# Spreading the normalisation factors of layer 1's first pass: 32 transposed rows and picking products in place of a widened copy

## The chip, the cores and the metric

The kernel runs on one core of a Trainium2 chip. The time is device time in microseconds (us), from one execution of the whole program; the number given for a kernel is the median of its runs. A core has engines that run side by side, each with its own queue of instructions in order: TensorE (PE in the profile; PEld is its loading of weights), VectorE (DVE), ScalarE (ACT), GpSimd (POOL), and SyncE (SP), which issues the transfers here. They wait for each other through semaphores.

## The reference

The input x is (4, 64, 256, 256) in fp32: four images, 64 channels, 256 rows and columns. Layer 0 is a gated convolution with a small Fourier filter; layer 1 runs two state-space blocks over the pixels, one along rows and one along columns. What the change concerns is the entry of layer 1, where each pixel is normalised over its 64 channels, once for each of the two directions, with the same mean and variance and different gains:

```python
def _layer_norm(x, g, b):
    mu = jnp.mean(x, axis=-1, keepdims=True)
    var = jnp.mean((x - mu) ** 2, axis=-1, keepdims=True)
    return (x - mu) * jax.lax.rsqrt(var + EPS) * g + b

def _s5_block(x, i, ...):
    fx = _layer_norm(x, ln1_g[i], ln1_b[i])
    h = _s5_scan(fx, ...)          # a linear recurrence along the sequence, both ways
    x = jax.nn.gelu(h) + fx
    fx2 = _layer_norm(x, ln2_g[i], ln2_b[i])
    return fx2 @ ff_enc[i].T @ ff_dec[i].T + fx2

x = x + layer0(_gn(x))             # _gn: normalisation over groups of 2 channels
x = x + layer1(_gn(x))             # y_h over rows, y_v over columns, then a 1x1 fusion
```

So one factor, rsqrt(var + EPS), belongs to each pixel, and it multiplies all 64 channels of that pixel.

## The kernel before

Layer 0 takes the first 4.18 ms of the profiled execution. Layer 1 then handles the four images one after the other. For each it runs `pass_a`, `scan` and `pass_b`. `pass_a` normalises the image, stores the result in DRAM for `pass_b`, and forms the summaries of 16 pixels that `scan` turns into carried states.

`pass_a` cuts an image into 16 strips of 16 rows (NS1 = 16). A strip lies in SBUF as 128 partitions (64 channels of one half of the rows, 64 of the other) by 8 rows of 256 pixels, and is worked on as four blocks i = 0 to 3 of 512 columns. The steps of a strip are these, with the names that the profile shows:

- `centre(g, i)`: a product of the block with the matrix `cenr` takes out the mean over the channels (PSUM tile `pc`, two banks). ScalarE copies it to `xc` and squares it to `sq`.
- `sums`: products of `sq` with a narrow matrix write the variances into PSUM tile `pv`, as 32 columns of TensorE for each block. ScalarE copies them to `sums`.
- `rstd_of`: four transposes bring them to 128 pixels by 32 (again `pv`; two factors for each of 4 x 4 pieces), VectorE adds EPS (`ve`), and GpSimd raises them to the power -1/2 (`rs`, 128 x 32).
- `widen`: one VectorE copy repeats each of the 32 factors 64 times, once for each channel: `rw`, 128 x 2048, one buffer.
- `affine(g, i)`: four transposes of 128 x 128 pieces of `rw` lay the factors out as channels by pixels (PSUM tile `pr`, two banks), and VectorE multiplies them with `xc` into `z`.
- `scaled_in`: ScalarE applies the gains and biases of the two directions (`fv`, `fh`); `store` sends both to DRAM.
- `mirrored`, `summary_columns`, `summary_rows`, `place_columns`, `place_rows`: sums and differences of mirrored pixels (`sd`, by VectorE for one direction and GpSimd for the other), products with `wa` (PSUM tiles `pt` and `ps`), a copy `m` by ScalarE, and VectorE's writes into the states `sf` and `sb`.

The order of work on each engine is written out by hand. The loop over n runs 20 times and mixes the steps of five strips: `centre` works on strip n, `sums`, `rstd_of` and `widen` on strip n - 1, `affine` on strip n - 2, the rest on strips n - 3 and n - 4. Nothing is reordered, since `tc.keep_in_program_order` fixes each engine's order. At the end of an iteration stand

```python
                at(n - 2, affine, 3)
                ...
                at(n - 3, summary_columns, n - 3, 0)
                at(n - 1, widen)
                at(n - 3, mirrored, 0)
```

and the next iteration begins with `centre(n, 0)` and `affine(n - 2, 0)`, which reads what `widen` wrote just before. On TensorE a steady iteration is: `pc`, `pr`, `pv` (sums), `pt`, `pc`, `pr`, `pv` (transposes), `ps`, `pc`, `pr`, `ps`, `pc`, `pr`, `pt`. An fp32 product is two TensorE instructions in the profile (two passes over the moving columns), a transpose is one.

In the profile's lines, L1096 is the helper that records a product, L1100 the one that records a transpose, and L301 and L162 are the helpers behind nearly all VectorE, ScalarE and GpSimd operations in order, so those are told apart by their tiles.

Of the kernel before, what the change touches and what calls it, by code (L numbers as in the profile page):

```python
# [16 lines left out]
C = 64  # L17
HID = 170
S = 256
P = 128  # L20
# [88 lines left out]
def tile_kernel(ctx: ExitStack, tc: tile.TileContext, x, cst, w0, winp, wdwp, w1, out):  # L109
    nc = tc.nc  # L110
    nb = x.shape[0]

    def new(pool, shape, tag, bufs=None, dt=F32):
        return pool.tile(shape, dt, tag=tag, name=tag, **({} if bufs is None else {"bufs": bufs}))
# [9 lines left out]
    def con(name):  # L124
        o, w = CONST_AT[name]
        return ct[:, o : o + w] if o < CONST_0 else tables[0][:, o - CONST_0 : o - CONST_0 + w]

    ident, swap, nswap = con("ident"), con("swap"), con("nswap")
# [6 lines left out]
    def group_norm(mv, psum, tag, keep, bank=(512,)):  # L135

        ps = new(psum, [P, *bank], tag)
        ps = ps[:, 0] if len(bank) > 1 else ps
        nc.tensor.matmul(ps[:, 0:1], lhsT=con("gm"), rhs=mv[:, 0:1], start=True, stop=True)
        nm = new(gpool, [P, 1], f"nm{keep}")  # L140
        nc.vector.tensor_scalar(nm, ps[:, 0:1], -1.0, None, ALU.mult)
        dev = new(gpool, [P, 1], "dev")
        nc.vector.tensor_tensor(dev, mv[:, 0:1], nm, ALU.add)
        var = new(gpool, [P, 1], "var")
        nc.vector.scalar_tensor_tensor(var, dev, dev, mv[:, 1:2], ALU.mult, ALU.add)
        ps2 = new(psum, [P, *bank], tag)
        ps2 = ps2[:, 0] if len(bank) > 1 else ps2
        nc.tensor.matmul(ps2[:, 0:1], lhsT=con("gm"), rhs=var, start=True, stop=True)
        ve = new(gpool, [P, 1], "ve")
        nc.vector.tensor_scalar(ve, ps2[:, 0:1], GN_EPS, None, ALU.add)  # L150
        rs = new(gpool, [P, 1], f"rs{keep}")
        nc.gpsimd.tensor_tensor(rs, ve, mhalf[:, 0:1], ALU.pow)
        return nm, rs
# [10 lines left out]
    vec, act, gps = InOrder(nc.vector), InOrder(nc.scalar), InOrder(nc.gpsimd)  # L164
# [27 lines left out]
    with ExitStack() as l0:  # L192
        wp = l0.enter_context(tc.tile_pool(name="w0", bufs=1))
# [16 lines left out]
        for h in range(2):  # L210
            p = slice(h * C, (h + 1) * C)
# [39 lines left out]
        with tc.tile_pool(name="pssp", bufs=1, space=PSUM) as pp:  # L251
            ps = new(pp, [P, 512], "sp")
# [23 lines left out]
        with ExitStack() as l1w:  # L276
# [31 lines left out]
            vec = Paced()  # L308
# [3 lines left out]
            def tmp(n=2, dt=F32):  # L312
                n_tmp[0] += 1
                return new(sp, [P, n], f"tmp{n_tmp[0]}", None, dt)
# [49 lines left out]
            def mul(a, b):  # L364
                o = tmp()
                TT(o, a, b, ALU.mult)
                return o
# [76 lines left out]
            for d in range(2):  # L444
# [28 lines left out]
                if d == 1:  # L473
# [18 lines left out]
                    for f in range(2):  # L492
                        o = wtb[1][:, at_e + 8 * f : at_e + 8 * f + 8].rearrange("p a (h c) -> p (a h) c", h=2)
                        group(o, 16, c1[f], c2[f], ec_r, ec_i, place)
                else:
# [6 lines left out]
                    for f in range(2):  # L502
                        o = wtb[0][:, at_r + 8 * f : at_r + 8 * f + 8].rearrange("p a (h c) -> p (a h) c", h=2)
# [40 lines left out]
            u, t, r, i = mul(ur, ur), mul(ui, ui), tmp(), tmp()  # L544
# [9 lines left out]
            n = 1  # L554
# [26 lines left out]
            for d in range(2):  # L581
                w = lambda name, d=d: wts[d][:, W1_AT[name][0] : W1_AT[name][0] + W1_AT[name][1]]
                ps = new(pw, [P, 512], "pw")
# [9 lines left out]
            for d in range(2):  # L593
                ps = new(pw, [P, 512], "pw")
# [7 lines left out]
                for h in range(2):  # L602
                    p = slice(h * C, (h + 1) * C)
                    TS(wos[d][p, p], mts[d][p, 0, :], par(d, "g2")[p], None, ALU.mult)
            burst[1]()
            for d in range(2):
                mm(
                    psb[:, 0:1], lhsT=mts[d][0:C].rearrange("p h c -> p (h c)"), rhs=par(d, "b2")[0:C],
                    start=(d == 0), stop=(d == 1),
                )  # L610
                ps = new(pw, [P, 512], "pw")
# [14 lines left out]
        pp = l0.enter_context(tc.tile_pool(name="ps0", bufs=2, space=PSUM))  # L626
        wk = l0.enter_context(tc.tile_pool(name="wk0", bufs=2))
# [316 lines left out]
        for b in range(nb):  # L944
            if b + 1 < nb:
                nxt_stats = new(wk, [P, 2 * NS0, 6], "stats1")
            for s in range(NS0):
                n = b * NS0 + s
# [116 lines left out]
    def load_strip(b, s):  # L1065
        t = new(ring, [P, 8, S], "strip")
        for h, r, row in rows_of(s):
            nc.sync.dma_start(out=t[h, r], in_=x1d[b][:, row : row + 7 : 2, :])
        return t
# [3 lines left out]
    with tc.tile_pool(name="psn", bufs=2, space=PSUM) as pn:  # L1073
        for b in range(nb):
            nm, rs = group_norm(moments2[b], pn, "pn", "1")
# [3 lines left out]
            ps = new(pn, [P, 512], "pn")  # L1079
# [3 lines left out]
    def pass_a(b, x0):  # L1083
        with ExitStack() as es:
            wp = es.enter_context(tc.tile_pool(name="wa", bufs=1))
            wk = es.enter_context(tc.tile_pool(name="wka", bufs=2))
            pp = es.enter_context(tc.tile_pool(name="psa", bufs=2, space=PSUM))
# [3 lines left out]
            rs, off = norms[:, b, 0:1], norms[:, b, 1:2]  # L1091
            cen = new(wp, [P, P], "cenr")
            nc.vector.tensor_scalar(cen, con("cen"), rs, None, ALU.mult)

            def mm(*args, **kw):
                tc.keep_in_program_order(nc.tensor.matmul(*args, **kw))  # L1096

            def turn_blocks(ps, v):
                for k in range(4):
                    tc.keep_in_program_order(nc.tensor.transpose(ps[:, k * P : (k + 1) * P], v(k), ident))  # L1100

            def centre(g, i):
                ps = new(pp, [P, 512], "pc")
                mm(ps, lhsT=cen, rhs=g["x"][:, 2 * i : 2 * i + 2, :].rearrange("p a b -> p (a b)"), start=True, stop=True)
                xc, sq = new(wk, [P, 512], "xc", 10), new(wk, [P, 512], "sq", 5)
                act.activation(xc, ps, AF.Identity, bias=off)
                act.activation(sq, ps, AF.Square, bias=off)
                g["xc", i], g["sq", i] = xc, sq

            def sums(g):  # L1110

                ps = new(pp, [P, 512], "pv", 1)
                for i in range(4):
                    mm(ps[32 * i : 32 * i + 32], lhsT=con("on2")[:, 2:34], rhs=g.pop(("sq", i)), start=True, stop=True)
                g["sums"] = new(wk, [P, 512], "sums", 1)
                act.copy(g["sums"], ps)
# [7 lines left out]
                gps.tensor_tensor(r, ve.rearrange("p n c -> p (n c)"), mhalf, ALU.pow)  # L1124
                g["rs"] = r

            def widen(g):

                g["r"] = new(wk, [P, 32, C], "rw", 1)
                vec.tensor_copy(g["r"], g.pop("rs").unsqueeze(2).to_broadcast([P, 32, C]))  # L1130

            def affine(g, i):

                if i == 0:
                    g["fv"], g["fh"] = new(wk, [P, 8, 256], "fv"), new(wk, [P, 16, 128], "fh")
                ps, z = new(pp, [P, 512], "pr"), new(wk, [P, 2, 16, 16], "z", 3)
                turn_blocks(ps, lambda k: g["r"][:, 8 * k + 2 * i : 8 * k + 2 * i + 2].rearrange("p a c -> p (a c)"))
                vec.tensor_tensor(
                    z.rearrange("p r q g -> p r g q"), g.pop(("xc", i)).rearrange("p (r g q) -> p r g q", r=2, q=16),
                    ps.rearrange("p (r g q) -> p r g q", r=2, q=16), ALU.mult,  # L1140
                )
                g["z", i] = z
# [23 lines left out]
            def summary_columns(g, s, k):  # L1166
                if k == 0:
                    g["pc"] = new(pp, [P, 512], "pt", 1)
                ps, sd = g["pc"], g.pop(("sd", 1, k))
                for r in range(4):  # L1170
                    mm(
                        ps[:, k * 256 : (k + 1) * 256], lhsT=wa[1][:, k * 4 + r], rhs=sd[:, r], start=(r == 0),
                        stop=(r == 3),
                    )
                if k == 1:
                    g["mc"] = new(wk, [P, 256], "m")
                    act.copy(g["mc"], ps[:, 256:])
# [34 lines left out]
            def at(s, step, *args):  # L1212
                if 0 <= s < NS1:
                    step(got[s], *args)

            for n in range(NS1 + 4):
                if n + 1 < NS1:
                    got[n + 1] = {"x": load_strip(b, n + 1)}
                at(n, centre, 0)
                at(n - 2, affine, 0)  # L1220
                at(n - 1, sums)
                at(n - 2, scaled_in, 0)
                at(n - 3, mirrored, 1)
                at(n - 4, summary_columns, n - 4, 1)
                at(n, centre, 1)
                at(n - 2, affine, 1)
                at(n - 1, rstd_of)
                at(n - 2, scaled_in, 1)
                at(n - 4, place_columns, n - 4)
                at(n - 4, summary_rows, n - 4, 0)  # L1230
                at(n, centre, 2)
                at(n - 2, affine, 2)
                at(n - 2, scaled_in, 2)
                at(n - 4, summary_rows, n - 4, 1)
                at(n, centre, 3)
                at(n - 2, affine, 3)
                at(n - 4, place_rows, n - 4)
                at(n - 2, scaled_in, 3)
                at(n - 2, store, n - 2)
                at(n - 3, summary_columns, n - 3, 0)  # L1240
                at(n - 1, widen)
                at(n - 3, mirrored, 0)

    def scan(tabs):
# [299 lines left out]
    for b in range(nb):  # L1544
        pass_a(b, first)
        first = pass_b(b)
# [77 lines left out]
```

## Time and profile before

| What | us |
|---|---|
| Median of 3 runs (lowest to highest) | 9118.38 (9117.01 to 9126.76) |
| The profiled execution's own time | 9128.26 |
| Its span, first to last instruction | 9126.5 |
| Granted TensorE clock, mean | 0.986 of full |
| Stretches with the four `pass_a` (each with some us around it) | 318, 306, 290, 315 |
| TensorE busy in them | 256.7, 246.5, 246.2, 257.8 |
| TensorE idle ahead of the transposes of `rw`, all four | 181.2 |
| 64 copies into `rw`, median of one | 3.234 |

The profile is of one execution, which took 9.9 us more than the median run. A TensorE matmul's end in it is modelled, and neighbouring matmuls overlap, so times of TensorE work are best read from one start to the next. Busy shares are averages over stages with different limits; the stage that matters here is `pass_a`, some 1.2 ms in all.

### The profile page before, as it was taken

How to read it: one execution, taken by the hardware profiler on the slowest of the kernel's cores; microseconds unless marked ns; L12 is line 12 of the kernel's file. 1: busy time of each engine (PE TensorE's matmuls, PEld its weight loads, DVE VectorE, ACT ScalarE, POOL GpSimd, SP SyncE). 2: the span in 40 equal slices, each digit the busy share in tenths (PEclk: the TensorE clock that was granted, in tenths of full speed). 3: DMA queues.
4: the chain of work that ended last, by engine and by line, in shares of the span. 5: the costliest groups of instructions: out<-in, count | busy, mean ns of one | idle time of the engine just before them, and what ended most of it. 6: DMA issues, size and time to landing. Idle time of an engine off the chain costs nothing. (4 is left out here: it accounts for less than half of the span.)

```text
span 9126.5 us, 182410 instructions
## 1 busy us (share of the span) xinstructions
PE 8613.1 (94%) x78454; PEld 5705.4 (63%) x78454; DVE 7105.8 (78%) x8837; ACT 3460.7 (38%) x5218; POOL 2406.8 (26%) x1278
## 2 busy tenths in 40 slices
PE   3999999999999999998899988999978999889999
PEld 2666666666666666665566656566655666555666
DVE  7999999999999998896766756677756677567676
ACT  3444444444444444445422236222254222352222
POOL 3000000000000000003734435544446444455443
PEclk9999999999999999999999999999999999999999
DMA  7444444444444333334423335233253233451332
GB/s 175 107 107 107 104 105 110 109 103 105 108 107 107 92 93 87 91 85 134 147 57 88 85 103 177 73 80 88 70 170 113 70 89 80 117 187 40 88 84 70
DMA packets 655573, 938.37 MB, mean 103 GB/s; under 512 B 43184, under 2 KB 584880, under 8 KB 619184
## 3 DMA queue, kind: packets, MB, share of 16 engines
q1 hardware_dynamic: 654768, 926.71, 38.3%
q8 instruction: 618, 10.13, 0.5%
q14 instruction: 187, 1.53, 0.1%
HBM read 583.86 MB, written 275.05 MB: 94 GB/s over the span
## 5 line engine op out<-in xcount | busy, mean ns | idle before, releaser
L205 PE MATMUL m<-v,sw 64*128 64x256 f32 (+1 forms) x8192 | 1538.6, 392 | 0.1
L205 PEld LDWEIGHTS m<-v,sw 64*128 64x128 f32 (+1 forms) x8192 | 1120.0, 187 | 503.2 <-issue 360.0
L1439 POOL TENSOR_TENSOR xr<-xr,fx 128x512 f32<-128x512 f32 x512 | 651.5, 1272 | 1864.4 <-ACT xr L1438 1375.5
L1344 PE MATMUL pst<-fx,wb 64*128 64x256 f32 (+1 forms) x4992 | 1019.8, 438 | 37.8 <-DVE stm L301 18.3
L692 POOL MEMSET at<- 64x256 f32 x4 | 1.2, 308 | 3685.1 <-PE two L205 3685.1
L301 DVE SCALAR_TENSOR_TENSOR acc<-xat,taps,acc 128x1024 f32<-128x1024 f32 x640 | 820.6, 1282 | 15.3 <-ACT acc L162 1.6
L1344 PEld LDWEIGHTS pst<-fx,wb 64*128 64x128 f32 (+1 forms) x4992 | 508.9, 187 | 374.6 <-issue 245.3
L1469 POOL TENSOR_TENSOR rs<-ve,mhalf 128x32 f32<-128x32 f32 x128 | 695.5, 5434 | 100.5 <-DVE ve L301 100.5
L162 ACT ACTIVATE ge<-two 128x1024 f32<-128x1024 f32 x256 | 262.7, 1026 | 1080.1 <-PE two L205 1080.0
L301 DVE SCALAR_TENSOR_TENSOR stm<-stm,step,pst 128x512 f32<-128x512 f32 x640 | 478.6, 748 | 232.5 <-PE pst L1344 219.0
L1440 ACT ACTIVATE sq<-xr 128x512 f32<-128x512 f32 x512 | 323.4, 632 | 876.4 <-POOL xr L1439 876.4
L205 PEld LDWEIGHTS m<-ct,hw 128*64 128x64 f32 x16384 | 509.3, 138 | 118.1 <-issue 118.1
L301 DVE SCALAR_TENSOR_TENSOR sto<-sto,step,pst 128x512 f32<-128x512 f32 x512 | 382.9, 748 | 242.5 <-PE pst L1344 231.2
L1344 PE MATMUL px<-wb,xr 128*128 128x128 f32 x4096 | 567.8, 282 | 0.0
L301 DVE TENSOR_TENSOR z<-xc,pr 128x512 f32<-128x512 f32 x256 | 265.1, 1037 | 386.2 <-PE pr L1100 378.8
L301 DVE TENSOR_TENSOR hw<-two,wsp 128x1020 f32<-128x1020 f32 (+1 forms) x384 | 422.7, 1101 | 176.0 <-PE two L205 162.7
L1344 PEld LDWEIGHTS px<-wb,xr 128*128 128x128 f32 x4096 | 518.0, 192 | 54.2 <-issue 41.8
L301 DVE TENSOR_TENSOR y<-px,rs 128x512 f32<-128x512 f32 x512 | 354.2, 692 | 226.5 <-PE px L1344 217.2
L1344 PE MATMUL ph<-sto,wb 128*64 128x128 f32 (+1 forms) x5120 | 528.0, 299 | 0.0
L205 PE MATMUL m<-ct,hw 128*64 128x64 f32 x16384 | 527.1, 223 | 0.0
L1344 PE MATMUL ph<-stm,wb 128*64 128x128 f32 (+1 forms) x5120 | 525.0, 299 | 0.0
L1344 PEld LDWEIGHTS ph<-stm,wb 128*64 128x64 f32 (+1 forms) x5120 | 408.9, 147 | 144.6 <-issue 128.0
(317 smaller groups left out, 16420.7 us busy)
## 6 DMA issues: line engine op xcount, KB each, us to landing
strip<-x1d SPq DMA_DIRECT2D x512, 256.0 KB, 7.5
fx<-fxd SPq DMA_DIRECT2D x128, 1024.0 KB, 7.0
at<-in_x_dram SPq DMA_DIRECT2D x248, 320.0 KB, 5.4
xen<-xat SPq DMA_DIRECT2D x256, 258.0 KB, 4.8
sx<-in_x_dram SPq DMA_DIRECT2D x256, 256.0 KB, 4.0
pr<-in_x_dram SPq DMA_DIRECT2D x256, 256.0 KB, 4.1
er<-in_x_dram SPq DMA_DIRECT2D x256, 256.0 KB, 4.1
x1d<-x SPq DMA_DIRECT2D x256, 256.0 KB, 4.0
```

The source lines that it names most:

```text
L162: return lambda *args, **kw: tc.keep_in_program_order(getattr(self.engine, name)(*args, **kw))
L205: tc.keep_in_program_order(nc.tensor.matmul(*args, **kw))
L301: tc.keep_in_program_order(getattr(nc.vector, name)(*args, **kw))
L692: nc.gpsimd.memset(at[C:P, 4, 1 : S + 1], 0.0)
L1344: tc.keep_in_program_order(nc.tensor.matmul(*args, **kw))
L1439: nc.gpsimd.tensor_tensor(xr, xr, fx, ALU.add)
L1440: nc.scalar.activation(sq, xr, AF.Square)
L1469: nc.gpsimd.tensor_tensor(r, ve.rearrange("p n c -> p (n c)"), mhalf, ALU.pow)
```

## The change

`widen` and the tile `rw` are gone. In their place `lay` transposes the factors once, from 128 pixels x 32 to 32 rows x 128 pixels (PSUM tile `pv`), and ScalarE copies that to the new tile `rt` (32 x 128). `affine` then no longer transposes; it forms four products per block. The stationary operand is a slice of a constant `pick`, 32 rows by 128 columns, that holds a one where a channel's column belongs to the row in question, and the moving operand is `rt`. Each product thereby copies two of the 32 rows to 64 channels each, into the same place of `pr` as before. `pick` is written once at the start of each `pass_a` by a VectorE copy of a 32 x 32 identity, spread 64 times.

The place in the order changes too: `lay` stands ahead of `summary_columns(n - 3, 0)`, where `widen` stood behind it. In the built program TensorE's steady iteration reads: `pc`, `pr`, `pv` (sums), `pt`, `pc`, `pr`, `pv` (transposes), `ps`, `pc`, `pr`, `ps`, `pc`, `pr`, `pv` (the new transpose), `pt`. ScalarE's new copy stands between the last `fh` of one iteration and the first `xc` of the next.

```diff
             cen = new(wp, [P, P], "cenr")
             nc.vector.tensor_scalar(cen, con("cen"), rs, None, ALU.mult)
 
+            pick = new(wp, [32, 32, C], "pick")
+            nc.vector.tensor_copy(pick, ident[0:32, 0:32].unsqueeze(2).to_broadcast([32, 32, C]))
+
@@
-            def widen(g):
-
-                g["r"] = new(wk, [P, 32, C], "rw", 1)
-                vec.tensor_copy(g["r"], g.pop("rs").unsqueeze(2).to_broadcast([P, 32, C]))
+            def lay(g):
+
+                ps = new(pp, [P, 512], "pv", 1)
+                tc.keep_in_program_order(nc.tensor.transpose(ps[0:32, :P], g.pop("rs"), ident))
+                g["r"] = new(wk, [32, P], "rt")
+                act.copy(g["r"], ps[0:32, :P])
@@
                 ps, z = new(pp, [P, 512], "pr"), new(wk, [P, 2, 16, 16], "z", 3)
-                turn_blocks(ps, lambda k: g["r"][:, 8 * k + 2 * i : 8 * k + 2 * i + 2].rearrange("p a c -> p (a c)"))
+                for k in range(4):
+                    o = 8 * k + 2 * i
+                    mm(
+                        ps[:, k * P : (k + 1) * P], lhsT=pick[:, o : o + 2].rearrange("p a c -> p (a c)"), rhs=g["r"],
+                        start=True, stop=True,
+                    )
@@
                 at(n - 2, scaled_in, 3)
                 at(n - 2, store, n - 2)
+                at(n - 1, lay)
                 at(n - 3, summary_columns, n - 3, 0)
-                at(n - 1, widen)
                 at(n - 3, mirrored, 0)
```

## The prediction

> **What bounds the kernel now.** I read the groups of TensorE first, then the tile `rw`, then one steady iteration of `pass_a` in order of time, then the clock by stretches. The page's first rows and the groups by form:
>
> ```profile
> PE 8613.1 (94%) x78454; PEld 5705.4 (63%) x78454; DVE 7105.8 (78%) x8837; ACT 3460.7 (38%) x5218; POOL 2406.8 (26%) x1278
> ...
> L1100 PE MATMUL pr<-ct,rw 128*128 128x128 f32 x1024 | 168.3, 290 | 181.2 <-DVE rw L301 181.0
> ```
>
> TensorE is the fullest engine, and in `pass_a` its one large idle place is ahead of these transposes: 181 us over 64 strips, ended by VectorE's copy. The same in time order (start, length, what, idle before):
>
> ```profile
> 4290.84 1.02 PE L1096 MATMUL pc<-strip,cenr 128*128 128x512 f32 x2
> 4294.37 0.63 PE L1100 MATMUL pr<-ct,rw 128*128 128x128 f32 x4 [2.51 <-DVE rw L301]
> 4294.93 1.06 PE L1096 MATMUL pv<-sq,ct 128*32 128x512 f32 x8
> ...
> 4297.76 1.02 PE L1096 MATMUL pc<-strip,cenr 128*128 128x512 f32 x2
> 4298.62 0.60 PE L1100 MATMUL pr<-ct,rw 128*128 128x128 f32 x4
> 4299.05 0.60 PE L1100 MATMUL pv<-ct,sums 128*128 128x128 f32 x4
> 4299.58 2.06 PE L1096 MATMUL ps<-sd,wa 64*128 64x128 f32 x32
> 4301.57 1.12 PE L1096 MATMUL pc<-strip,cenr 128*128 128x512 f32 x2
> 4302.53 0.60 PE L1100 MATMUL pr<-ct,rw 128*128 128x128 f32 x4
> 4303.06 2.06 PE L1096 MATMUL ps<-sd,wa 64*128 64x128 f32 x32
> ...
> 4306.01 0.60 PE L1100 MATMUL pr<-ct,rw 128*128 128x128 f32 x4
> 4306.44 1.89 PE L1096 MATMUL pt<-sd,wa 128*128 128x256 f32 x8
> 4308.17 1.02 PE L1096 MATMUL pc<-strip,cenr 128*128 128x512 f32 x2
> ```
>
> Three things are to be seen. An iteration takes 4308.17 - 4290.84 = 17.33 us; without the wait it is dense. The wait, from start to start, is 4294.37 - 4290.84 - 0.86 (a `pc` without one, 4297.76 to 4298.62) = 2.67, so TensorE's own work is 14.66. And a change of array shape costs: four transposes take 0.43 where the next group has the same shape (4298.62, 4306.01) but 0.53 ahead of the 64-row `ps` (4299.05, 4302.53), and a `pc` takes 0.96 behind a `ps` against 0.86: 0.10 to leave a shape plus 0.10 in the first instruction of the next, 0.20 per change. Six changes are in the 14.66.
>
> The wait has a second price. Clock by stretches of 3.41 us (PE busy first, PEclk the sixth figure):
>
> ```profile
> 4256.03:4259.44 3.41, 1.37 (x12) 0.58 (x12) 2.60 (x2) 0.76 (x2) 0.81 (x1) 1.00 1.00 402
> 4259.44:4262.86 3.42, 3.42 (x11) 2.50 (x8) 2.50 (x3) 2.00 (x3) 0.00 (x0) 0.50 1.01 315
> 4262.86:4266.27 3.41, 3.41 (x36) 2.67 (x36) 1.68 (x4) 2.25 (x4) 0.54 (x1) 1.00 0.25 47
> ```
>
> A stretch mostly filled by the wait is followed by one at half clock, which costs about 1.65 us. By the starts of the 64 `rw` copies, each pass has two short first intervals (12.7 to 14.2), twelve middle ones and one last. Of the 48 middle ones 32 take about 17.33 and sixteen 18.7 to 19.0; together 857.5 us, mean 17.86. The last ones take 17.25, 14.63, 17.51 and 17.45.
>
> **What the Trainium skill says.** TensorEngine Tiling (Array Packing), Key Properties: changing the tiling mode, not just the tile, drains TensorE. The trace agrees: the 0.20 above. TensorE: Matmul & The Clock Gate, Why this matters for your kernels: one product over 32 rows takes as long as one over 128. No run here has 32 rows; 64-row `ps` pairs take (2.0 - 0.2)/16 = 0.11 a pass, like 128 rows. The same page, What's actually happening: the clock halves after a free-running window of 3413 ns without enough work. The windows shown agree. TensorEngine Tiling, Feature Incompatibilities: column tiling and the fp32 transpose mode exclude each other. The new transpose has 32 output rows; nothing here shows one.
>
> **The change, part by part,** for a steady iteration.
>
> *Copy and wait.* VectorE loses 3.23 us, which matters only through the wait; -2.67 on TensorE, and the half-clock windows behind it.
>
> *Transposes to products.* A transpose is one instruction, 0.109 (0.43/4). An fp32 product of this size is two: in the last pass `px`, four such products, has
>
> ```profile
> 4752.60 1.05 PE L1344 MATMUL px<-wb,xr 128*128 128x128 f32 x8
> 4753.49 0.60 PE L1462 MATMUL pv<-ct,sums 128*128 128x128 f32 x4
> ```
>
> 0.89 for eight, 0.112 each. Four groups an iteration: 4 x (0.896 - 0.436) = +1.84.
>
> *Changes of shape.* The products use 32 rows. Changes per iteration become 13: `pc` to `pr` four times, `pr` to each follower four times, sums to `pt`, transposes to `ps`, two `ps` to `pc`, new transpose to `pt`. Seven more, 7 x 0.20 = +1.40. The trace has no 32-row group, so this is bounded by 0 (no drain) and 0.20; I take 0.20, since both shapes it shows (64 rows, 32 columns) cost that.
>
> *New transpose.* One instruction, +0.11 (0.22 if it needs two passes); its changes are counted.
>
> Sum on TensorE: 14.66 + 1.84 + 1.40 + 0.11 = 18.01. The transposing group behind the wait (4294.37 to 4294.93) is 0.03 longer than the others for starting cold, and that goes too: about 17.96.
>
> *New wait.* TensorE's first `pr` of the next iteration needs `rt`. Behind the fourth `pr` (start = 0), VectorE's `z` starts 0.31 after the last of its eight instructions (as 4306.01 to 4306.65 shows for four), 1.20; `fv` 1.08 later (4306.65 to 4307.73), `fh` +0.72, `rt` +0.78 (the place of `xc` now, 4308.45 to 4309.23): 3.79. The copy is an estimate of 0.25 from `m` (256 columns, 0.36) and `sums` (512, 0.586), then 0.14 to TensorE as from `rw`: 4.18. TensorE itself needs products 1.09, new transpose 0.31, `pt` 1.83, `pc` 0.95: 4.18. So the wait is about 0 to 0.1. Queued behind `rt` on ScalarE are `xc` and `sq`; their next reader is far off. The new transpose waits for GpSimd's `rs`: done 6.8 us after the `pv` transposes began (4305.82 against 4299.05), needed 8.9 after. Covered; if not, all of TensorE stands behind it.
>
> So an iteration takes about 18.0: 0.67 more than an undisturbed one of before, 0.7 to 1.0 less than a disturbed one.
>
> *Over a pass.* Middle: 48 x 18.0 = 864 against 857.5, **+6.5**. Last interval: no `pc`, so 17.96 - 4.0 for four of them - 0.4 for two changes that vanish = 13.6, plus 0.95 in which `rt` is late without the cover of a `pc`: 14.5 against a mean of 16.7, 4 x -2.2 = **-8.8**. After it VectorE loses a copy of 2.73 beside GpSimd's `sd`, for which TensorE waited 2.85; most is taken back by longer `pr`: 4 x -0.7 = **-2.8**, rough. First two intervals: bound by `rs` (5.43 on GpSimd) and half clock in both kernels. There `rw` took 1.23 (GpSimd idle), about what the new path needs; but the products of blocks 0 and 1 lie in the chain to the next `rs`, and the new transpose holds `pc` behind it: an estimate of 1 to 2.5 per pass, 4 x 2 = **+8**. `pick` (as long as that 1.23 `rw`) delays the first image's constants, **+1**; in the other passes VectorE is otherwise idle there. `sums` needs `pv`'s one buffer, free once `rt` is read, which `pr` waits for anyway. No DMA is added; stores and loads keep their places with SP.
>
> Sum: 6.5 - 8.8 - 2.8 + 8 + 1 = **+4**. On the profiled execution 9128.3 + 4 = 9132, on the median, 9.9 lower, **9122**: no change that counts. A measurement of this kernel can tell about 0.2% (18 us) from none.
>
> **Rivals.**
>
> *Cheaper changes of shape.* If entering 32 rows costs half of what 64 rows do, seven changes save 0.7 an iteration, 64 x 0.7 = 45: 9077. For it: no 32-row row exists. Against: the two shapes shown cost the same. It decides below 0.15 per change (22 us over 64 iterations).
>
> *Products that cannot load ahead (the other side).* In a 32-row shape all products sit in one row group. If the next weights can't be loaded behind the running product, a pass takes the 0.19 of a weight load, not 0.112: 8 x 0.078 x 256 groups = 160, 9282. Against: `ps` reaches 0.11 with two row groups, each loaded ahead of itself. It decides from small sizes: 14 us more, a pass of 0.119, already makes the kernel slower by over 0.2%.
>
> *`rt` late or the clock still halved.* If ScalarE's chain is 0.4 longer than added up, or half-clock windows go on at half the former number, it is 64 x 0.4 = 26 or 8 x 1.65 = 13 more: 9135 to 9148. The chain has no slack, which speaks for it.
>
> *The transfers bound it.* Then nothing would move, 9118. Against: the engines wait for each other, not for `strip`, in the iteration shown.
>
> **How the numbers follow.** Forecast 0.57, its own range 9105 to 9139 (0.3 an iteration either way); cheaper changes 0.17; late `rt` or clock 0.16; no loading ahead, in part or whole, 0.10. Taking in most of the late `rt` and the near part of the cheaper changes, the range is 9098 to 9150. Faster by over 0.2%: 0.18, the cheaper changes and the forecast's edge. Slower: 0.26, no loading ahead and late `rt`, with the edge. Within: 0.56.
>
> **What would show it.** `pr` groups of eight with 0.112 steps and a `pc` of 0.95; 13 changes; idle before `pr` near 0.1, ended by ScalarE's `rt`; iterations even at 18.0 with no half clock in the middle of a pass; last ones near 14.5. An iteration of 17.3 or less, or one over 18.4, proves the sum wrong.

## The result and the profile after

| | before | after |
|---|---|---|
| Median, us (lowest to highest of 8 runs) | 9121.65 (9117.01 to 9131.79) | 9147.02 (9142.35 to 9150.26) |
| Ratio after to before, 95% interval | | 1.0026 [1.0017, 1.0036] |
| The profiled execution's own time | 9128.26 | 9142.35 |
| Its span | 9126.5 | 9140.5 |

The change makes the kernel slower by 0.26%, 25 us between the medians. The two profiled executions lie 14.1 us apart: the one of after is the fastest of its eight runs, and the one of before is above its median. The traces can therefore place 14 us; the other 11 are spread of the runs that no single trace shows.

First the page's row of TensorE, and then its groups by form (busy time in us and mean ns of one; then, after the last bar, the idle time ahead of the group and what ended it):

```profile
PE 8797.8 (96%) x79542; PEld 5834.6 (64%) x79542; DVE 6923.1 (76%) x8777; ACT 3469.1 (38%) x5282; POOL 2390.3 (26%) x1278
```

```profile
L1099 PE MATMUL pr<-rt,pick 32*128 32x128 f32 x2048 | 313.2, 294 | 11.1 <-ACT rt L162 9.8
L1099 PE MATMUL pc<-strip,cenr 128*128 128x512 f32 x512 | 308.3, 691 | 24.2 <-DMA strip<-x1d 20.0 <-DVE strip L301 3.5 <-DVE norms L1081 0.2
...
L1133 PE MATMUL pv<-ct,rs 128*32 128x128 f32 x64 | 18.9, 295 | 22.2 <-POOL rs L162 22.2
```

The change did what it says. TensorE stood idle 181.2 us ahead of `pr` before; it now stands 11.1, of which 9.8 are ended by ScalarE's `rt`. The idle time has not moved to another reader in like measure: 22.2 us stand before the new transpose, ten times in all, at the starts of the passes. Yet TensorE is busier by 184.7 us on the page, more than the idle time that went. A steady iteration in order of time (start, length, what):

```profile
4295.15 0.28 PE L1133 MATMUL pv<-ct,rs 128*32 128x128 f32 x1
4295.27 1.89 PE L1099 MATMUL pt<-sd,wa 128*128 128x256 f32 x8
4296.99 1.02 PE L1099 MATMUL pc<-strip,cenr 128*128 128x512 f32 x2
4298.05 1.15 PE L1099 MATMUL pr<-rt,pick 32*128 32x128 f32 x8
4299.14 1.06 PE L1099 MATMUL pv<-sq,ct 128*32 128x512 f32 x8
4300.13 1.99 PE L1099 MATMUL pt<-sd,wa 128*128 128x256 f32 x8
4301.96 1.02 PE L1099 MATMUL pc<-strip,cenr 128*128 128x512 f32 x2
4302.91 1.15 PE L1099 MATMUL pr<-rt,pick 32*128 32x128 f32 x8
4304.00 0.66 PE L1103 MATMUL pv<-ct,sums 128*128 128x128 f32 x4
4304.59 2.06 PE L1099 MATMUL ps<-sd,wa 64*128 64x128 f32 x32
...
4311.75 1.15 PE L1099 MATMUL pr<-rt,pick 32*128 32x128 f32 x8
4312.83 0.28 PE L1133 MATMUL pv<-ct,rs 128*32 128x128 f32 x1
4312.95 1.89 PE L1099 MATMUL pt<-sd,wa 128*128 128x256 f32 x8
```

From one new transpose to the next, 4312.83 - 4295.15 = 17.68. From the third of a pass on, every interval but the last takes 17.67 to 17.69, in all four passes, where before sixteen of the middle ones took 18.7 to 19.0. So the middle of a pass became faster. The loss is at the starts of the passes, and the clock by stretches of 3.41 us shows it (length; then busy time of PE, PEld, DVE, ACT, POOL; then PEclk, the granted clock, where 0.50 is half clock; then the DMA's share and GB/s). These are stretches of after, at the start of its first pass:

```profile
4204.05:4207.46 3.41, 0.93 (x3) 0.37 (x3) 0.00 (x0) 0.26 (x1) 2.42 (x1) 1.00 0.96 226
4207.46:4210.88 3.42, 3.42 (x17) 1.98 (x16) 0.91 (x1) 1.27 (x2) 0.00 (x0) 0.50 0.44 81
4210.88:4214.29 3.41, 3.41 (x9) 1.13 (x6) 0.11 (x1) 2.44 (x4) 0.00 (x0) 0.50 0.00 0
...
4217.70:4221.12 3.42, 3.42 (x10) 2.28 (x10) 0.53 (x1) 1.98 (x4) 3.42 (x1) 0.50 0.00 0
...
4234.77:4238.19 3.42, 3.42 (x10) 1.69 (x10) 1.21 (x2) 1.62 (x3) 1.47 (x1) 0.50 0.00 0
4238.19:4241.60 3.41, 3.16 (x18) 2.09 (x18) 1.18 (x2) 2.40 (x4) 3.41 (x1) 1.00 0.00 0
```

Two lines ask for attention. The first stretch holds a wait for GpSimd's `rs` (the new transpose at 4206.53 had 3.81 us of idle time ahead of it), and the next runs at half clock; that happened before the change too. But then TensorE is busy for nine stretches, eight of them to the full, and the clock stays at 0.50 for 30.7 us. Before the change the same place looks like this:

```profile
4208.24:4211.66 3.42, 0.21 (x2) 0.21 (x3) 1.23 (x1) 0.86 (x2) 1.89 (x1) 1.00 1.09 251
4211.66:4215.07 3.41, 3.41 (x13) 1.05 (x12) 1.01 (x1) 0.70 (x2) 0.00 (x0) 0.50 0.22 42
4215.07:4218.48 3.41, 3.41 (x18) 2.12 (x17) 1.51 (x3) 3.41 (x6) 1.06 (x1) 1.00 0.00 0
```

One busy stretch, and full clock is back. Here is the sum over the four passes, in us, from these marks: the first `pc` of a pass, the starts of the first `pr` of each of the 16 strips, and GpSimd's first operation of `scan`.

| Four passes | to first `pr` | first 2 intervals | 12 middle | last | to `scan` | all | of it at half clock |
|---|---|---|---|---|---|---|---|
| before | 99.7 | 117.7 | 857.0 | 64.9 | 108.3 | 1247.6 | 171.1 |
| after | 97.6 | 144.5 | 848.7 | 58.8 | 107.8 | 1257.5 | 155.4 |
| difference | -2.1 | +26.8 | -8.3 | -6.1 | -0.5 | +9.9 | |

All 155.4 us of half clock in after lie ahead of the third strip's `pr`; before, 83.0 lay there and 88.1 later. The difference arises once the new products run: from the first strip's `pr` to the third's it is 105.6 against 45.8. Within the passes of before, each of the 28 stretches at half clock that TensorE filled (busy for at least 3.38 us) was followed by full clock; of the 32 such stretches in after, 20 were followed by more half clock, and all 20 hold work of `pr`. The remaining 4.1 of the 14 us between the spans fall outside the passes.

### The profile page after: what moved, and what is told of

Read it like the earlier page. It is cut to its first block, busy times and chain, and to the rows that moved or that the text cites. A ratio compares the mean times of both kernels' runs of the same rounds, so it can differ in the third digit from the quotient of the medians.

```text
span 9140.5 us, 184745 instructions
## 1 busy us (share of the span) xinstructions
PE 8797.8 (96%) x79542; PEld 5834.6 (64%) x79542; DVE 6923.1 (76%) x8777; ACT 3469.1 (38%) x5282; POOL 2390.3 (26%) x1278
## 5 line engine op out<-in xcount | busy, mean ns | idle before, releaser
L1479 POOL TENSOR_TENSOR rs<-ve,mhalf 128x32 f32<-128x32 f32 x128 | 695.3, 5432 | 99.8 <-DVE ve L301 99.8
L162 POOL TENSOR_TENSOR rs<-ve,mhalf 128x32 f32<-128x32 f32 x64 | 347.7, 5432 | 589.8 <-DVE ve L301 578.4
```

The source lines that it names most:

```text
L162: return lambda *args, **kw: tc.keep_in_program_order(getattr(self.engine, name)(*args, **kw))
L1479: nc.gpsimd.tensor_tensor(r, ve.rearrange("p n c -> p (n c)"), mhalf, ALU.pow)
```

## The experiments

Two questions were open: what keeps the clock at half, and whether the starts lose by the clock at all. Three theories stood in the expectations. T1: the clock's measure of activity gives products over 32 rows little credit. T2: the added changes of array shape, each with its drain (the 0.20 us a change that the prediction charges), count as idle time. T3: it isn't the clock; `pc` merely stands behind the new transpose, and the products lie in the chain to the next `rs`.

### 128 rows, by zeros

`pick` and `rt` get 128 rows, of which 96 are zero. The product is the same, and the array is used over all its rows, so that neither a 32-row shape nor a change toward it is left.

```diff
-            pick = new(wp, [32, 32, C], "pick")
-            nc.vector.tensor_copy(pick, ident[0:32, 0:32].unsqueeze(2)...)
+            pick = new(wp, [128, 32, C], "pick")
+            nc.gpsimd.memset(pick, 0.0)
+            nc.vector.tensor_copy(pick[0:32], ident[0:32, 0:32].unsqueeze(2)...)
+            rts = [new(wp, [128, P], f"rt{k}") for k in range(2)]
+            for t in rts:
+                nc.gpsimd.memset(t, 0.0)
+            laid = [0]
...
-                g["r"] = new(wk, [32, P], "rt")
-                act.copy(g["r"], ps[0:32, :P])
+                g["r"], laid[0] = rts[laid[0] % 2], laid[0] + 1
+                act.copy(g["r"][0:32], ps[0:32, :P])
```

> The picking products run over 128 rows: pick and rt are padded with rows of zeros, so the products, their number and their results stay the same, but TensorE's shape is that of centre's products. Theory 1 (the clock monitor gives little credit to products over 32 rows, so TensorE stays at half clock for some 30 us at the start of each pass): half-clock stretches at the starts shrink to single ones of 3.4 us as in the kernel before, the first two intervals between rt copies fall from 36 us together to under 30. Theory 2 (it is the many drains between shapes that read as idle): the same. Theory 3 (the start is slow because pc stands behind the new transpose and the products lie in the chain to the next factor, not because of the clock): the first two intervals stay above 33 us. All: a middle iteration falls from 17.68 to about 17.1 (seven drains fewer, rt then late by 0.4). Time under 1 and 2 about 9086, under 3 about 9118.

Measured: 9075.73 us (9074.37 to 9076.81), ratio to before 0.9951 [0.9936, 0.9966]. The clock by stretches at the start of its first pass:

```profile
4204.08:4207.49 3.41, 0.95 (x3) 0.56 (x4) 0.00 (x0) 0.27 (x2) 2.41 (x1) 1.00 0.98 219
4207.49:4210.91 3.42, 3.42 (x17) 1.81 (x15) 1.01 (x1) 1.26 (x2) 0.00 (x0) 0.50 0.45 88
4210.91:4214.32 3.41, 3.41 (x21) 2.20 (x18) 1.03 (x2) 2.96 (x5) 0.00 (x0) 1.00 0.00 0
```

The wait ahead of it is nearly the same as in after (0.95 busy against 0.93), and so is the busy stretch that follows. Here full clock is back after it, and the first two intervals of the passes fell from 144.5 to 117.6. The iteration fell from 17.68 to 16.95; in it TensorE waits 0.29 for `rt` against 0.11, and its first `pr` behind that wait is 0.10 slower than the others. T3 alone can't explain the starts, but T1 and T2 both can, since the drains went too.

### 128 rows, but the changes of shape kept

The kernel with 128 rows, and each product is split into two over 64 columns, so that the array still changes its shape ahead of `pr` and behind it.

```diff
-                    mm(
-                        ps[:, k * P : (k + 1) * P], lhsT=pick[:, o : o + 2]..., rhs=g["r"],
-                        start=True, stop=True,
-                    )
+                    for a in range(2):
+                        mm(
+                            ps[a * C : (a + 1) * C, k * P : (k + 1) * P], lhsT=pick[:, o + a], rhs=g["r"],
+                            start=True, stop=True,
+                        )
```

> Padded to 128 rows as well, but each product is split into two of 64 columns that run side by side, so the shape is 128 rows by 64 columns and every drain of the changed kernel remains. Theory 1 (rows in use count): the starts recover, first two intervals under 31 us together; middle iterations stay near 17.7; time about 9115. Theory 2 (drains count): half clock for some 30 us at the starts as in the changed kernel, time about 9147. Theory 3: as in the changed kernel too, without a link to the clock.

Measured: 9107.9 us (9103.56 to 9113.84), ratio 0.9983 [0.9976, 0.9990]. In the profile 16 products of 64 columns take 1.03 with their drain, like eight of 128 columns, so two run at a time and the array is as full as with 128 columns:

```profile
4298.46 1.02 PE L1104 MATMUL pc<-strip,cenr 128*128 128x512 f32 x2
4299.41 1.09 PE L1104 MATMUL pr<-rt,pick 128*64 128x128 f32 x16
4300.44 0.66 PE L1108 MATMUL pv<-ct,sums 128*128 128x128 f32 x4
```

A stretch with a wait at its pass start, and what follows:

```profile
4221.75:4225.16 3.41, 1.22 (x9) 0.41 (x5) 1.02 (x1) 3.41 (x6) 2.42 (x1) 1.00 0.82 181
4225.16:4228.58 3.42, 3.42 (x25) 1.78 (x24) 1.00 (x2) 1.54 (x4) 0.00 (x0) 0.50 1.06 368
4228.58:4231.99 3.41, 3.41 (x28) 1.84 (x24) 3.04 (x4) 2.84 (x5) 0.00 (x0) 1.00 0.97 369
```

The drains are there (a `pc` ahead of a `pr` takes 0.95, not the 0.86 of the run with 128 columns, and an iteration 17.45), and one busy stretch still brings full clock back, in all 15 filled stretches at half clock of its passes. The first two intervals take 119.8. T2 falls.

### 64 rows

The padded kernel with 64 in place of 128 rows in `pick` and `rt`.

```diff
-            pick = new(wp, [32, 32, C], "pick")
+            pick = new(wp, [64, 32, C], "pick")
...
+            rts = [new(wp, [64, P], f"rt{k}") for k in range(2)]
```

> Padded to 64 rows: drains as in the changed kernel but one (ahead of the second ps). Theory 1: half the array's rows in use give half the credit, so the half-clock stretch at the starts is shorter than with 32 rows, perhaps gone: first two intervals between 28 and 35 us. Theory 2: as in the changed kernel, 36 us. A middle iteration about 17.5. Time 9105 to 9137.

Measured: 9118.4 us (9110.76 to 9122.45), ratio 0.9995 [0.9987, 1.0004].

```profile
4221.77:4225.18 3.41, 1.66 (x7) 0.83 (x8) 0.76 (x1) 3.38 (x7) 1.64 (x1) 1.00 1.07 241
4225.18:4228.60 3.42, 3.42 (x16) 1.53 (x15) 2.10 (x3) 0.98 (x3) 0.00 (x0) 0.50 1.02 412
4228.60:4232.01 3.41, 3.41 (x10) 1.89 (x9) 1.11 (x1) 2.98 (x5) 0.00 (x0) 0.50 0.78 274
4232.01:4235.42 3.41, 3.41 (x10) 1.71 (x9) 1.21 (x2) 1.87 (x3) 1.71 (x1) 0.50 0.00 0
4235.42:4238.84 3.42, 3.04 (x18) 1.97 (x17) 1.31 (x2) 2.29 (x4) 3.42 (x1) 1.00 0.01 2
```

Here two filled stretches are followed by more half clock, before the third is followed by full clock. Over its passes 8 of 21 filled stretches at half clock were followed by another, where with 128 rows it was none of 13 and with 32 rows 20 of 32. Ahead of the third strip's `pr`, half clock adds up to 74.4 us with 128 rows, 112.5 with 64 and 155.4 with 32; the first two intervals take 117.6, 128.6 and 144.5.

### The 32 rows kept, the waits at the start filled

The kernel after, with further products over 128 rows during the first two waits for `rs` of a pass. They write a further tile `pt`, which nobody reads; nothing is left out.

```diff
+                if n in (1, 2):
+                    warm = new(pp, [P, 512], "pt", 1)
+                    for _ in range(4 if n == 1 else 3):
+                        mm(warm, lhsT=cen, rhs=wa[1][:, 0:4]..., start=True, stop=True)
                 at(n - 1, lay)
```

> The changed kernel with its 32-row products, and in the first two waits of a pass for the factors TensorE computes seven extra products of 128 rows by 512 columns into a PSUM bank that is not yet in use; nobody reads them. Theory 1: no window is empty there, the clock doesn't fall, and 32-row products at full clock don't make it fall (the middle of the pass shows that), so the starts run at full clock: first two intervals about 28 us together, time about 9117. Theory 2: the same, if the drains alone don't make it fall. Theory 3: the starts stay as slow or grow by the extra products, time 9147 to 9160.

Measured: 9114.21 us (9108.49 to 9118.9), ratio 0.9990 [0.9981, 0.9998]; 33 us less than after. The first two intervals of the passes fall from 144.5 to 113.8, while the middle stays at 849.2, with nearly every iteration at 17.68 (the first of each pass up to 17.91). The clock at the start, where after had 0.50 throughout:

```profile
4208.84:4212.26 3.42, 3.23 (x20) 1.51 (x20) 0.84 (x1) 1.52 (x3) 0.14 (x1) 1.00 0.82 162
4212.26:4215.67 3.41, 3.41 (x20) 1.93 (x16) 1.24 (x3) 3.19 (x6) 0.00 (x0) 1.00 0.00 0
4215.67:4219.08 3.41, 3.41 (x20) 2.25 (x19) 1.02 (x1) 3.41 (x6) 3.38 (x1) 1.00 0.00 0
```

More work, and less time: the starts are bound by the clock, and T3 as the whole cause falls. It also shows filled stretches with 32-row products that hold full clock once it is there.

### The same for the kernel before

If filling the waits (here three of them) helps the kernel before as much, the 32 rows aren't to blame.

```diff
+                if n in (1, 2, 3):
+                    warm = new(pp, [P, 512], "pt", 1)
+                    for _ in range((4, 4, 2)[n - 1]):
+                        mm(warm, lhsT=cen, rhs=wa[1][:, 0:4]..., start=True, stop=True)
                 at(n - 3, summary_columns, n - 3, 0)
```

> The kernel before the change, with 4, 4 and 2 further products over 128 rows into a tile that nobody reads, ahead of the summaries in the second, third and fourth iterations of a pass; nothing is left out. It asks what half clock at the starts of a pass costs the kernel before. T1: it had single windows there, so it gains little: 0 to 12 us, 9113 to 9125; the half-clock windows in the middle of its first passes stay, since they follow the waits for rw there. Rival (half clock at the starts costs both kernels alike, and the 32 rows are not to blame): 25 to 35 us less, about 9092, as much as the kernel after gained from the same products.

Measured: 9104.09 us (9095.76 to 9114.04), ratio 0.9980 [0.9973, 0.9986]. That lies between the two expectations and fits neither: half clock at the starts cost the kernel before as well, 19.5 us by the medians and 16.7 in the first two intervals (117.7 to 101.0), which is more than T1 had allowed it. The kernel after gained 33 and 30.7 from the like. And the waits for `rw` in the middle remain, with 78.5 us of half clock behind the third strip's `pr` (88.1 in the kernel before):

```profile
L1100 PE MATMUL pr<-ct,rw 128*128 128x128 f32 x1024 | 161.1, 281 | 152.2 <-DVE rw L301 152.2
```

This run gives the nearest comparison of the two kernels without half clock. With the waits filled, the first two intervals take 101.0 in the kernel before and 113.8 in the one after. The first interval of a pass is free of half clock in both, 11.24 against 12.63: 1.4 for the longer chain. The second is 13.94 against 15.11 at best, but there a stretch of half clock is left in the kernel after, at its third wait, so that up to 1.2 more may be the chain's. That makes 1.4 to 2.6 a pass, 6 to 10 in all. So of the 26.8 that the starts lost, 6 to 10 belong to the longer chain (T3's part) and 17 to 21 to the clock.

### Two further versions

With 128 rows TensorE waits 0.29 for `rt`. The first version moves the new transpose and its copy ahead of the last block's products, from the fourth iteration of a pass on:

```diff
                 at(n, centre, 3)
+                if n > 3:
+                    at(n - 1, lay)
                 at(n - 2, affine, 3)
...
-                at(n - 1, lay)
+                if n <= 3:
+                    at(n - 1, lay)
```

> The products over 128 rows again, and from the fourth iteration of a pass on the new transpose and its copy stand ahead of the last block's products instead of behind them; nothing is left out. In the former run with 128 rows an iteration took 16.95 us, of which TensorE stood about 0.3 before each first product, for ScalarE's copy rt. T1 (the rows in use set the clock at the starts, and in the middle only the order of the copy is left to gain): the wait before the first products goes, an iteration takes 16.6 to 16.7, 12 x 4 x 0.3 = 14 us less than the former run, about 9062. Rival: ScalarE's copy then stands ahead of fv and fh of the last block and holds them and the summaries behind them, or TensorE waits for rs at the earlier place; then 9075 or more, and the wait shows before the new transpose or before the last summaries' products.

Measured: 9053.37 us (9050.78 to 9055.77), ratio 0.9924 [0.9910, 0.9939]. Its group of `pr`:

```profile
L1104 PE MATMUL pr<-rt,pick 128*128 128x128 f32 x2048 | 278.2, 280 | 0.2
```

Next to no wait is left there. An iteration takes 16.56, so 0.39 went: the wait of 0.29 and the 0.10 of the slow first group behind it, of which the expectation had only the former. The rival's stall did not come.

The second version fills the waits at the start as well (4, 3 and 2 products).

> The kernel of the run beside it, with 4, 3 and 2 further products over 128 rows into a tile that nobody reads, ahead of the new transpose in the second, third and fourth iterations of a pass; nothing is left out. T1: the single half-clock windows left at the starts of a pass (3 to 4 of 3.4 us each, some 1.7 us of cost where TensorE sets the pace) go, 4 x 1.7 to 4 x 3.4 = 7 to 14 us less than without them, about 9050. Rival: the waits for rs there set the pace and TensorE's speed beside them does not matter, or the extra products delay the chain: 9060 to 9070.

Measured: 9033.14 us (9030.33 to 9038.76), ratio 0.9902 [0.9886, 0.9919], the fastest of all: 90.5 us below the kernel before in the same round (9123.64). The first two intervals fall from 116.5 to 102.8, and the time to the first `pr` by 2.2. The gain, 20 us by the medians and 15.9 in the passes, is above the 7 to 14 expected; so the waits for `rs` did not set the pace there alone. Since the two versions differ from the kernel after in several things at once, they show what can be had, and say little on the cause. One thing can be read from the second: its first two intervals have no half clock and the order of the kernel after, over 128 rows, and take 12.01 and 13.68, 0.5 a pass more than the 11.24 and 13.94 of the kernel before with filled waits. So of the 6 to 10 us put down to the longer chain above, only about 2 are the chain itself; the rest comes with the 32 rows, by the drains around them or by what half clock is left in that run.

## Why the prediction was right and wrong

The sum said +4 us, which was to mean no change; the median is 25 higher. The time lies inside the range given, but outside the 9105 to 9139 of the likeliest case. Two terms were wrong by 15 and 19 us, in opposite directions, and the range reaches to 9150 for the sake of a rival that did not come true; that it holds the measured time is in part luck.

| Step of the sum | forecast | measured |
|---|---|---|
| Middle intervals | +6.5 | -8.3 |
| First two intervals | +8 | +26.8 |
| Last interval | -8.8 | -6.1 |
| After it | -2.8 | -0.5 |
| `pick`, to the first `pr` | +1 | -2.1 |
| Outside the passes | 0 | +4.1 |
| Profiled execution | +4 | +14.1 |

**The wait and its half-clock windows: right.** The 2.67 of waiting per iteration went, and no half clock is left in the middle of a pass. The new wait for `rt` is 0.107 (4298.05 - 4296.99 = 1.06, against 0.95 at 4301.96), at the top of the 0 to 0.1, and the copy took 0.24 where 0.25 was estimated.

**Products for transposes: right.** Eight at 0.112 with an exit and an entry give the 1.09 of a group (4298.05 to 4299.14).

**Changes of array shape: mis-sized, by 0.3 an iteration.** The sum charged the new transpose 0.11 for itself and two changes of 0.10 each around it. Transpose to `pt` takes 4295.27 - 4295.15 = 0.12, and `pt` behind it 1.72, no longer than before: by these times the transpose with 32 output rows makes no change of shape, and only leaving `pr` is paid, in `pr`'s 1.09. Transposes behind a `pr` also enter at 0.06 in place of 0.10 (`pv` from `sums`: 0.59). TensorE's own work is thus 17.57 in place of 17.96, and with the wait an iteration is 17.68 instead of 18.0; times 48, that is the 15 us. (The prediction's own terms give 17.98; its 17.96 is a slip without weight.) The section Feature Incompatibilities of TensorEngine Tiling (Array Packing) in the Trainium skill, on which the prediction had based its doubt, has it that column tiling and the fp32 transpose exclude each other; the transpose ran with 32 output rows and, by these times, without a change of shape.

The run with 128 rows separates the terms: its own work is 16.66, which is 14.66 with +1.84 for the products and +0.11 for the transpose, within 0.05. The 32 rows add 0.91 to that, against the 1.40 charged, of which 0.3 were not due at the new transpose.

**First two intervals: the step that failed.** The prediction said these are "bound by `rs` (5.43 on GpSimd) and half clock in both kernels", and so priced only the longer chain, 1 to 2.5 a pass. The chain, with the drains around the products, came to 1.4 to 2.6, about what was forecast. What the step left out is that half clock doesn't end the same way in both kernels. It put half clock at the same in both, and in the trace of before a filled stretch ended it every time; but that trace had no product over 32 rows in it. With `pr` over 32 rows, half clock ahead of the third `pr` went from 83.0 to 155.4 us. The section What's actually happening of TensorE: Matmul & The Clock Gate in the Trainium skill has one busy window bring the full clock back; the trace of after shows seven windows full of work that did not, before the eighth did, and there the measurement decides.

**Last interval and what follows it: mis-sized.** 14.7 against 14.5 forecast is nearly right; the -8.8 came out at -6.1 mainly because the last intervals of before, counted from `pr` rather than from `rw`, take 16.2 and not 16.7. The -2.8 after it, called rough, was -0.5.

**The rivals.** Cheaper shape changes came true at one place only, the new transpose. Products that can't load ahead did not: 0.112 a step. The rival `rt` late or clock still halved gave 9135 to 9148, and the number fell there, yet by other means: `rt` is on time, and the half clock is not in the middle of the passes but at their starts. The transfers did not bound it: the middle of the passes moved with TensorE's work in every run.

## What to carry to other kernels

Where TensorE comes out of a wait at half clock, it was not enough here that it is busy; what it was busy with decided how soon it was fast again. Padding the small contraction with zero rows cost no TensorE time (a step stayed at 0.112), and it saved both the drains around the products and the slow starts, 71 us between the medians. A stall that can't be avoided can be worth filling with wide products that nobody reads, where TensorE's work behind it sets the pace (33, 20 and 20 us in the three runs here).

## What the runs showed of the hardware that was not expected

**Products over few rows delay the return to full clock.** Half clock ahead of the third strip's `pr` was 155.4, 112.5 and 74.4 us for 32, 64 and 128 rows. A product's duration is the same in all three, 0.112, and only zero rows were added. With 128 rows the changes of shape went too, but the pairs of 128 rows by 64 columns that run side by side kept them, and had 79.0. Within the trace of after, this is the busy time of `pr` alone in stretches at half clock and in the one that ends them, and PEclk:

```profile
4210.88:4214.29 3.41, 0.63 (x3) 0.50 0.00 0
...
4217.70:4221.12 3.42, 2.07 (x8) 0.50 0.00 0
...
4231.36:4234.77 3.41, 1.55 (x7) 0.50 0.70 204
4234.77:4238.19 3.42, 0.74 (x4) 0.50 0.00 0
4238.19:4241.60 3.41, 2.18 (x16) 1.00 0.00 0
```

All of the first four are filled. Those with 2.07 and 1.55 of `pr` are followed by more half clock, the one with 0.74 by full clock. But the one with 0.63 is followed by more half clock too. It also holds 0.85 of `pv` from `sq`, products over 128 rows and 32 columns, where the one with 0.74 holds only transposes in `pv`. So few columns seem to count as well, though less: in before the stretch at 4211.66 has 1.94 of the same `pv` and no 32-row product, and full clock follows.

So much is shown: products over few rows delay the return to full clock. Whether the hardware weighs rows, or cells, or something that goes with them is open; zero rows were enough, so it isn't the data. No run had 32 rows without the changes of shape.

**They lose full clock sooner, too.** In the passes of before, stretches at full clock with up to 1.40 us of TensorE work were followed by half clock, and all those with more than 1.45 by full clock. So a wait of some 2 us inside one stretch was enough there. With 128 rows padded by zeros one of 1.60 still lost it, with 64 rows one of 1.93. With 32 rows in after, a wait of 0.46 was enough:

```profile
5460.15:5463.56 3.41, 2.95 (x17) 1.88 (x16) 1.38 (x2) 2.19 (x5) 3.41 (x1) 1.00 0.04 5
5463.56:5466.98 3.42, 2.74 (x6) 1.17 (x6) 0.67 (x1) 3.42 (x8) 0.06 (x1) 0.50 1.06 237
```

Of the 2.95 us, 1.97 are `pr`. A filled stretch with 2.02 of `pr`, in the run with 32 rows and filled waits, kept full clock.

Whether a given wait falls into one stretch or is split by two depends on where the stretches begin. The first interval of the four passes of after, with the same work in each, took 19.56, 17.49, 15.77 and 17.49. That this also makes the spread between runs is a guess, which was not tested.
